# A decoder layer with routed experts: expert products scattered to token order by the tile and loaded plainly at the end, rows and sums in one buffer

## The chip, the cores and the metric

The kernel runs on one core of a Trainium2 chip. The metric is the time of one execution on the device in microseconds (us); the times shown are medians of several executions. A core has a matrix engine (TensorE, in profiles PE, with its weight loads listed apart as PEld), a vector engine (VectorE, DVE), a scalar engine (ScalarE, ACT), a general engine (GpSimd, POOL), and a queue engine (SyncE, SP) that issues transfers. Each engine takes its instructions in order; they wait for one another through semaphores. A transfer (DMA) issued by SP goes to one queue, one issued by POOL to others. An indirect transfer takes its row addresses from an index tile, one row for each of the 128 partitions.

## The reference

64 sequences of 128 tokens with 256 features go through one decoder layer, fp32 throughout: a state-space block, retention against a context, and a mixture of experts, each followed by a residual sum and a layer norm without gain. Cut to what matters:

```
x = _layernorm(x + attn(x))          # norm, W_in, conv, selective scan, W_out, + residual
x = _layernorm(x + xattn(x, ctx))    # q from x; k, v from ctx; scores * decay; no softmax
x = _layernorm(x + ffn(x))

def ffn(x):                          # shared expert + 2 of 8 routed experts per token
    shared = (silu(x @ sg.T) * (x @ su.T)) @ sd.T
    probs = sigmoid(x @ router_w.T + routing_bias)
    scores, indices = top_k(probs, 2)
    scores = scores / sum(scores, -1)
    w = zeros((t, 8)).at[arange(t)[:, None], indices].add(scores)
    g = silu(einsum('th,ehi->tei', x, gate_w)); u = einsum('th,ehi->tei', x, up_w)
    return shared + einsum('tei,eih,te->th', g * u, down_w, w)
```

## The kernel before

The rows of the decay table are equal in these inputs, so the function `_shared_decay` (L507) is used. The sequences are handled in 16 groups of 4 (512 tokens; a tile of a group is 128 partitions x 4 sequences x 256 features). The code is written as Python generators; `weave` (L1286) runs one as the main line and lets others step in between in proportion. The order so made is the order of each engine's queue.

**The loop** (L1319) has 17 ticks. Tick g runs the first half of group g (norm, input projection, convolution, scan), the second half of group g−1 (`after`: output projection, norm to x1, retention, norm to x2; then `route`), the shared expert of group g−2 (`early_shared`) unless the group is in `LATE` (groups 7 to 13), and expert tiles as far as their rows are known. `load_x` (L675) fetches x for the tick on POOL's queue with 2 buffers `xt`; the context tile `cT` is loaded in `after` (L857), also on POOL, and its buffer later holds the queries.

**Routing.** `route` picks two experts for each token, ranks the tokens of each expert, and scatters every x2 row to two rows of the DRAM array `xs`, which has one region for each expert: 8 indirect transfers a group (L1026), 128 in all. Positions are kept for the whole run in `index`, weights in `weight`. x2 of a late group, and x2 plus the shared expert's output of another, goes to the DRAM array `x2_rows`.

**Expert tiles.** `routed` runs 78 tiles: 57 of 256 rows, 21 of 128 rows. They become known in five batches (`BATCHES`, L41); `tile_list(k)` makes the list of batch k on the device: expert, first row, and whether new weights are needed. In the last batch each expert's last tile may be part empty, so the rows behind every expert's last are filled with zeros (L1098; the space behind the regions at the start, L621). For each tile `fetch` copies its entry (POOL, L1198), reads it into SP's registers, and loads the rows (L1201) and on a new expert 1.5 MB of weights (L1207). `hidden` transposes the rows, projects to gate and up, and multiplies; `down`, one tile later, projects down, copies the product out of PSUM (ACT, L1247) and stores it on SP to `ys` in tile order (L1248). 41 tiles run in the loop, 37 after it; with those `places` (L1156) steps along, which turns each scatter position in `index` into a row of `ys`.

**The last stage.** `all_shared` is the main line: for the 7 late groups it loads x2 back (`load_rows`, 4 buffers `x2_back`), transposes it and runs the shared expert. `all_sums` steps in between: for each group `combine` (L1264) gathers 8 times 128 rows of `ys` (POOL, L1270), each multiplied by its weight and added on DVE (L1274), then does the last layer norm into `o` and stores it. The 9 other groups come first in that list, the late ones follow as they are ready. `layernorm` (L626) takes statistics on DVE, one power on POOL (L636), one more on DVE, and applies the result on ACT a step later (L641).

PSUM has two pools: `gu` with 3 buffers for gate, up and the shared expert's output, `pm` with 5 for all else.

Of the kernel before, what the change touches and what calls it, by code (L numbers as in the profile page):

```python
# [42 lines left out]
NR = sum(n * r for _, _, n, r in BATCHES)  # L43
# [463 lines left out]
def _shared_decay(ctx, K):  # L507
# [84 lines left out]
    index = const.tile([P, NG * GB, 2], mybir.dt.int32, name="index")  # L592
    weight = const.tile([P, NG * GB, 2], F32, name="weight")

    x2_rows = dram.tile([NG, P, GB * D], F32, name="x2_rows", bufs=1)
    xs = dram.tile([NE * CAP + (NE - 1) * P, D], F32, name="xs", bufs=1)
    ys = dram.tile([NR, D], F32, name="ys", bufs=1)
# [13 lines left out]
    bounds = const.tile([P, NE, len(BATCHES)], F32, name="bounds")  # L611
    moves = const.tile([P, NE, len(BATCHES)], F32, name="moves")
    known = [0]
    weights = []
    for i in range(NW):
# [3 lines left out]
    zeros = const.tile([P, D], F32, name="zeros")  # L619
    nc.vector.memset(zeros, 0.0)  # L620
    nc.sync.dma_start(  # L621
        out=xs[NE * CAP :, :].rearrange("(i p) d -> p i d", p=P),
        in_=zeros.unsqueeze(1).to_broadcast([P, NE - 1, D]),
    )
# [50 lines left out]
    def load_x(g):  # L675
        xt = ring.tile([P, GB, D], F32, name="xt", bufs=2)
        nc.gpsimd.dma_start(out=xt, in_=x[g * GB : (g + 1) * GB].rearrange("b l d -> l b d"))
        return xt
# [173 lines left out]
    def after(g, st):  # L852
# [7 lines left out]
        x1 = one.tile([P, GB, D], F32, name="x1")  # L860
# [17 lines left out]
        def rotated(w, src, table, name, tag):  # L878

            ev = pm.tile([P, T], F32, name="pm")  # L880
            od = pm.tile([P, T], F32, name="pm")
            project(ev, w, 0, src)
            project(od, w, P, src)
            cos = rot_s[:, table, :].unsqueeze(1).to_broadcast([P, GB, L])
            sin = rot_s[:, table + 1, :].unsqueeze(1).to_broadcast([P, GB, L])
            r = one.tile([P, 2, T], F32, name=name, tag=tag)
            r0, r1 = seqs(r[:, 0, :]), seqs(r[:, 1, :])
            tmp = one.tile([P, GB, L], F32, name="tmp")
            nc.vector.tensor_tensor(r0, seqs(ev), cos, ALU.mult)
            nc.vector.tensor_tensor(tmp, seqs(od), sin, ALU.mult)  # L890
            nc.vector.tensor_tensor(r0, r0, tmp, ALU.subtract)
            nc.vector.tensor_tensor(r1, seqs(od), cos, ALU.mult)
            nc.vector.tensor_tensor(tmp, seqs(ev), sin, ALU.mult)
            nc.vector.tensor_tensor(r1, r1, tmp, ALU.add)
            return r
# [13 lines left out]
        qh = rotated(wq_s, x1T, 0, "qh", "cT")  # L909
# [9 lines left out]
        sc = one.tile([P, GB, L], F32, name="sc")  # L919
        nc.vector.tensor_tensor(sc, pss, dec.unsqueeze(1).to_broadcast([P, GB, L]), ALU.mult)  # L920
        yield
        x2 = ring.tile([P, GB, D], F32, name="x2", bufs=2)
# [10 lines left out]
        st["x2"] = x2  # L933

    writers = []

    def wrote(g, ins):

        tc.declare_no_dep(ins, group="scatters", reason="other rows")
        for k, (groups, *_) in enumerate(BATCHES):  # L940
            if groups <= g:
                tc.declare_no_dep(ins, group=f"fetches{k}", reason="other rows")
# [4 lines left out]
    def read(k, ins):  # L947

        tc.add_to_no_dep_group(f"fetches{k}", ins)
        for g in range(BATCHES[k][0], NG):  # L950
            tc.declare_no_dep(ins, group=f"scatters{g}", reason="other rows")
        for g, name in writers:
            if g < BATCHES[k][0]:
# [10 lines left out]
    def route(g, st):  # L964
# [46 lines left out]
        here = slice(g * GB, (g + 1) * GB)  # L1011
# [11 lines left out]
        nc.vector.tensor_copy(index[:, here, :], at)  # L1023
        for b in range(GB):
            for k in range(2):
                s = nc.gpsimd.indirect_dma_start(  # L1026
                    out=xs, in_=x2[:, b, :], in_offset=None,
                    out_offset=bass.IndirectOffsetOnAxis(ap=index[:, g * GB + b, k : k + 1], axis=0),
                )
                wrote(g, s.ins)  # L1030
        yield
# [6 lines left out]
        nc.vector.tensor_tensor(  # L1038
            weight[:, here, :], wk2, tot.unsqueeze(2).to_broadcast([P, GB, 2]), ALU.mult
        )  # L1040
        if g in LATE:
            nc.sync.dma_start(out=x2_rows[g], in_=x2.rearrange("p b d -> p (b d)"))
# [28 lines left out]
    def early_shared(g, st):  # L1071
        x2s = one.tile([P, GB, D], F32, name="x2s")
        yield from shared(st["x2"], st["x2T"], x2s)
        nc.sync.dma_start(out=x2_rows[g], in_=x2s.rearrange("p b d -> p (b d)"))

    def load_rows(g):
        t = late.tile([P, GB, D], F32, name="x2_back", bufs=4)
# [3 lines left out]
    def tile_list(k):  # L1081
# [5 lines left out]
        base = sum(m * r for _, _, m, r in BATCHES[:k])  # L1087
# [3 lines left out]
        if last:  # L1091

            behind = small.tile([P, NE], F32, name="behind", bufs=1)
            nc.vector.tensor_tensor(behind, pn, behind0, ALU.add)
            behind_i = small.tile([P, NE], mybir.dt.int32, name="behind_i", bufs=1)
            nc.vector.tensor_copy(behind_i, behind)
            for e in range(NE):
                s = nc.gpsimd.indirect_dma_start(  # L1098
                    out=xs, in_=zeros, in_offset=None,
                    out_offset=bass.IndirectOffsetOnAxis(ap=behind_i[:, e : e + 1], axis=0),  # L1100
                )
                wrote(groups - 1, s.ins)
# [18 lines left out]

        lo = bounds[:, :, k]
        nc.vector.tensor_tensor(lo, d, begin1, ALU.add)
        nc.vector.tensor_scalar(cum2[:, 0, :], cum0, float(size), float(base), ALU.mult, ALU.add)
        nc.vector.tensor_tensor(moves[:, :, k], cum2[:, 0, :], lo, ALU.subtract)
# [30 lines left out]
    def places():  # L1156

        n = NE * len(BATCHES)
        step = small.tile([P, n], F32, name="step", bufs=1)
        flat = moves.rearrange("p e k -> p (e k)")  # L1160
        nc.vector.tensor_copy(step[:, 0:1], flat[:, 0:1])
        nc.vector.tensor_tensor(step[:, 1:], flat[:, 1:], flat[:, 0 : n - 1], ALU.subtract)
        low = bounds.rearrange("p e k -> p (e k)")
        for g in range(NG):
            here = slice(g * GB, (g + 1) * GB)
            m = GB * 2
            was = small.tile([P, m], F32, name="was", bufs=1)
            nc.vector.tensor_copy(was, index[:, here, :].rearrange("p b k -> p (b k)"))
            over = small.tile([P, m, n], F32, name="over", bufs=1)
            nc.vector.tensor_tensor(  # L1170
                over, was.unsqueeze(2).to_broadcast([P, m, n]), low.unsqueeze(1).to_broadcast([P, m, n]), ALU.is_ge
            )
            nc.vector.tensor_tensor(over, over, step.unsqueeze(1).to_broadcast([P, m, n]), ALU.mult)
            by = small.tile([P, m], F32, name="by", bufs=1)
            nc.vector.tensor_reduce(by, over, AX.X, ALU.add)
            nc.vector.tensor_tensor(
                index[:, here, :].rearrange("p b k -> p (b k)"), was, by, ALU.add
            )
            yield

    def routed():
# [3 lines left out]
        def shape(i):  # L1185

            row = 0
            for k, (_, first, n, size) in enumerate(BATCHES):
                if i < first + n:
                    return k, size, row + (i - first) * size  # L1190
                row += n * size

        def fetch(i):

            k, size, _ = shape(i)
            t = tiles.tile([P, 2 * D + 4], F32, name="rows_in", bufs=3)
            entry = t[0:1, 2 * D : 2 * D + 3].bitcast(mybir.dt.int32)
            nc.gpsimd.tensor_copy(entry, what[:, i, :])  # L1198
            r = nc.sync.value_load(entry[:, 1:2], min_val=0, max_val=xs.shape[0] - size)
            t = t[:, 0 : size // P * D].rearrange("p (i d) -> p i d", d=D)  # L1200
# [12 lines left out]
        def hidden(i, t):  # L1213
            size = shape(i)[1]
# [8 lines left out]
            nc.scalar.copy(tT, ps)  # L1223
            yield
# [13 lines left out]
            return hid  # L1238

        def down(i, hid):  # L1240
            _, size, row = shape(i)
            wd = weights[i % NW][:, 2 * SZ :].rearrange("p (c h) -> p c h", c=CF)
            ps = pm.tile([P, size // P, D], F32, name="pm")
            for j in range(size // P):
                project_rows(ps[:, j, :], [h[:, j * P : (j + 1) * P] for h in hid], wd, slice(0, D))
            y = tiles.tile([P, size // P, D], F32, name="rows_out", bufs=2)
            nc.scalar.copy(y, ps)  # L1247
            nc.sync.dma_start(out=ys[row : row + size, :].rearrange("(j p) d -> p j d", p=P), in_=y)  # L1248

        ahead, waiting = [], None  # L1250
        for i in range(NT):
            if not ahead:
                ahead.append(fetch(i))
            hc = yield from hidden(i, ahead.pop(0))
            if waiting:
                down(*waiting)
            waiting = (i, hc)
# [6 lines left out]
    def combine(g, x2s):  # L1264

        for b in range(GB):
            s = g * GB + b
            for k in range(2):
                y = late.tile([P, D], F32, name="picked", bufs=12)
                nc.gpsimd.indirect_dma_start(  # L1270
                    out=y, out_offset=None, in_=ys,
                    in_offset=bass.IndirectOffsetOnAxis(ap=index[:, s, k : k + 1], axis=0),
                )
                nc.vector.scalar_tensor_tensor(  # L1274
                    x2s[:, b, :], y, weight[:, s, k : k + 1], x2s[:, b, :], ALU.mult, ALU.add
                )
            yield
        o = late.tile([P, GB, D], F32, name="o", bufs=2)
        yield from layernorm(o, x2s)
        nc.sync.dma_start(out=out[g * GB : (g + 1) * GB].rearrange("b l d -> l b d"), in_=o)  # L1280
# [67 lines left out]
    weave(rows, 6 * BATCHES[-2][2] + 4 * BATCHES[-1][2], (places(), NG, True))  # L1348
# [184 lines left out]
```

## Time and profile before

| what | value |
|---|---|
| median of 3 runs | 2128.95 us (2126.19 to 2129.11) |
| the profiled execution's own time | 2129.57 us |
| its span | 2127.9 us |
| PE busy | 1962.9 us (92%) |
| DVE, ACT, POOL busy | 1045.0, 744.4, 430.6 us |
| traffic | 244.85 MB, 115 GB/s in the mean |
| loop ends, about | 1530 us |
| tiles end, about | 1878.5 us |
| indirect transfers | 128 scatters of rows, 8 of zeros, 128 gathers |

The span is what the profile covers of the execution; the few tenths of a per cent around it are launch and end. In the page's second part each digit is the busy share of a fortieth of the span (53.2 us) in tenths. Groups name an instruction by line, engine and operation, output and inputs. The transfers that matter here, with KB each and the median time from issue to landing where it could be told:

```profile
xt<-in_x_dram POOLq DMA_DIRECT2D x16, 512.0 KB, 4.4
cT<-in_ctxT_dram POOLq DMA_DIRECT2D x16, 512.0 KB, 4.7
...
x_back<-x_rows SPq DMA_DIRECT2D x16, 512.0 KB
out_dram<-o SPq DMA_DIRECT2D x16, 512.0 KB
...
xs<-x,index POOLq DMA_INDIRECT x128, 2.5
picked<-ys,index POOLq DMA_INDIRECT x128, 2.8
```

POOL's longest waits, in total, times, and the longest one:

```profile
POOL rows_in L1198 <- PE pm L1221: 386.6, 44, 27.9
POOL cT L857 <- PE pm L914: 259.7, 9, 33.9
POOL cT L857 <- PE pm L1221: 193.8, 6, 32.3
...
POOL xt L677 <- DVE x L868: 72.1, 12, 19.9
```

### The profile page before, as it was taken

The page shows a single profiled execution, that of the slowest core. Times are in us where ns is not written, and L with a number is a line of the kernel's source. Part 1 is how long each engine was busy: PE and PEld are TensorE (multiplying, and loading weights), DVE is VectorE, ACT ScalarE, POOL GpSimd, SP SyncE. Part 2 cuts the span into 40 slices and gives each one's busy share as a digit, 9 for nine tenths or more (in the row PEclk, how much of TensorE's full clock was granted, in tenths as well). Part 3 has the DMA queues.
Part 4 walks back from the last instruction along what each step waited for, and adds up shares of the span by engine and source line. Part 5 has one row for each costly group of instructions (what it writes and reads, how often), then busy time and mean ns, then how long its engine had stood idle before and what let it go on. Part 6 is the DMA issues. An engine that isn't in the chain of part 4 may idle for free. (4 is left out here: it accounts for less than half of the span.)

```text
span 2127.9 us, 25170 instructions
## 1 busy us (share of the span) xinstructions
PE 1962.9 (92%) x8748; PEld 1420.9 (67%) x8748; DVE 1045.0 (49%) x2557; ACT 744.4 (35%) x1181; POOL 430.6 (20%) x504
## 2 busy tenths in 40 slices
PE   4799999999999999999999999999999998967767
PEld 1555666576766777776868676777878887844434
DVE  3666677565555655445555555454731111124453
ACT  2444344343342425353444435341211221212222
POOL 3031222121220202020211121110300000046671
PEclk9899999999999999999999999999999999999888
DMA  4111111331321334242524332233354567425441
GB/s 130 31 51 50 40 61 56 136 98 44 106 89 61 110 105 164 69 150 91 167 79 150 107 122 90 100 120 98 131 201 165 198 206 278 145 83 177 151 149 46
DMA packets 100888, 244.85 MB, mean 115 GB/s; under 512 B 23184, under 2 KB 68752, under 8 KB 91792
## 3 DMA queue, kind: packets, MB, share of 16 engines
q1 hardware_dynamic: 77968, 188.94, 26.6%
q0 software_dynamic: 17280, 51.40, 7.6%
q10 hardware_dynamic: 5504, 2.81, 0.5%
q8 instruction: 71, 1.16, 0.2%
q14 instruction: 65, 0.53, 0.1%
HBM read 202.48 MB, written 54.79 MB: 121 GB/s over the span
## 5 line engine op out<-in xcount | busy, mean ns | idle before, releaser
L664 PE MATMUL gu<-rows_T,routed_w 128*128 128x256 f32 (+1 forms) x2496 | 510.3, 356 | 9.1 <-ACT rows_T L1223 5.4
L664 PEld LDWEIGHTS gu<-rows_T,routed_w 128*128 128x128 f32 x2496 | 418.8, 192 | 77.4 <-issue 20.2
L1236 DVE TENSOR_TENSOR hid<-hid,gu 128x512 f32<-128x512 f32 x135 | 92.5, 685 | 358.6 <-PE gu L664 353.0
L664 PE MATMUL gu<-x2T,shared_w 128*128 128x512 f32 x512 | 239.4, 613 | 25.9 <-ACT x2T L652 16.2
L673 PE MATMUL pm<-routed_w,hid 128*128 128x256 f32 x1080 | 251.4, 381 | 11.6 <-DVE hid L1236 11.6
L664 PE MATMUL pm<-xnT,w_in_s 128*128 128x512 f32 x512 | 241.1, 597 | 0.7 <-ACT xnT L654 0.7
L673 PEld LDWEIGHTS pm<-routed_w,hid 128*128 128x128 f32 x1080 | 201.3, 190 | 46.0 <-DVE hid L1236 15.8
L664 PEld LDWEIGHTS gu<-x2T,shared_w 128*128 128x128 f32 x512 | 96.6, 195 | 142.6 <-issue 101.8
L702 DVE SCALAR_TENSOR_TENSOR xc<-pm,cw,xc 128x508 f32<-128x508 f32 (+2 forms) x192 | 140.3, 740 | 69.5 <-ACT xc L697 66.5
L1026 POOL DMA_INDIRECT xs<-x,index x128 | 137.4, 1073 | 170.6 <-DVE tot L1037 57.0
L1235 ACT ACTIVATE hid<-gu 128x512 f32<-128x512 f32 x135 | 80.4, 596 | 252.9 <-PE gu L664 252.7
L673 PE MATMUL gu<-shared_w,hc 128*128 128x256 f32 x512 | 128.3, 403 | 38.6 <-DVE hc L1058 38.6
L664 PEld LDWEIGHTS pm<-xnT,w_in_s 128*128 128x128 f32 x512 | 96.1, 192 | 84.1 <-issue 72.8
L1270 POOL DMA_INDIRECT picked<-ys,index x128 | 125.5, 981 | 104.7 <-DMA ys<-rows_out 31.0
L673 PEld LDWEIGHTS gu<-shared_w,hc 128*128 128x128 f32 x512 | 100.9, 202 | 64.7 <-DVE hc L1058 45.8
L1247 ACT COPY rows_out<-pm 128x512 f32<-128x512 f32 (+1 forms) x78 | 41.2, 528 | 265.7 <-PE pm L673 264.3
L1198 POOL COPY rows_in<-what 1x3 int32<-1x3 int32 x78 | 14.3, 188 | 502.1 <-PE pm L1221 386.6
L673 PE MATMUL pm<-w_out_s,sz 128*128 128x256 f32 x512 | 114.9, 380 | 0.4 <-DVE sz L848 0.3
L673 PEld LDWEIGHTS pm<-w_out_s,sz 128*128 128x128 f32 x512 | 96.5, 190 | 15.6 <-PE pm L841 1.3
L857 POOL DMA_DIRECT2D cT<-in_ctxT_dram x16 | 12.4, 776 | 453.5 <-PE pm L914 259.7
L636 POOL TENSOR_TENSOR rstd<-var,mhalf 128x4 f32<-128x4 f32 x64 | 65.9, 1030 | 166.2 <-DVE var L634 95.0
L697 ACT ACTIVATE xc<-pm,cb,cw 128x512 f32<-128x512 f32 x64 | 49.4, 773 | 112.5 <-PE pm L664 112.5
(225 smaller groups left out, 2629.9 us busy)
## 6 DMA issues: line engine op xcount, KB each, us to landing
routed_w<-in_ffn_dram SPq DMA_DIRECT2D x78, 1536.0 KB
rows_in<-xs SPq DMA_DIRECT2D x57, 256.0 KB
ys<-rows_out SPq DMA_DIRECT2D x57, 256.0 KB
xt<-in_x_dram POOLq DMA_DIRECT2D x16, 512.0 KB, 4.4
cT<-in_ctxT_dram POOLq DMA_DIRECT2D x16, 512.0 KB, 4.7
cq<-chunks SPq DMA_DIRECT2D x16, 512.0 KB
x_back<-x_rows SPq DMA_DIRECT2D x16, 512.0 KB
out_dram<-o SPq DMA_DIRECT2D x16, 512.0 KB
```

The costliest lines, as they stand in the source:

```text
L636: nc.gpsimd.tensor_tensor(rstd, var, mhalf, ALU.pow)
L664: nc.tensor.matmul(ps, lhsT=w[:, k, col : col + P], rhs=src[:, k, :], start=(k == 0), stop=(k == KD - 1),)
L673: nc.tensor.matmul(ps, lhsT=src[k], rhs=w[:, k, cols], start=(k == 0), stop=(k == chunks - 1))
L697: nc.scalar.activation(xcf[:, c, :], ps, AF.Identity, bias=cb[:, c : c + 1], scale=cw[:, c, TAPS - 1 : TAPS],)
L702: nc.vector.scalar_tensor_tensor(xc[:, c, :, s:], ps3[:, :, : L - s], cw[:, c, TAPS - 1 - s : TAPS - s], xc[:, c, :, s:], ALU.mult, ALU.add,)
L857: nc.gpsimd.dma_start(out=cT, in_=ctxT[:, g * T : (g + 1) * T].rearrange("(k p) t -> p k t", p=P))
L1026: s = nc.gpsimd.indirect_dma_start(out=xs, in_=x2[:, b, :], in_offset=None, out_offset=bass.IndirectOffsetOnAxis(ap=index[:, g * GB + b, k ...
L1198: nc.gpsimd.tensor_copy(entry, what[:, i, :])
L1235: nc.scalar.activation(hc, psg, AF.Silu)
L1236: nc.vector.tensor_tensor(hc, hc, psu, ALU.mult)
L1247: nc.scalar.copy(y, ps)
L1270: nc.gpsimd.indirect_dma_start(out=y, out_offset=None, in_=ys, in_offset=bass.IndirectOffsetOnAxis(ap=index[:, s, k : k + 1], axis=0),)
```

## The change

- **Rows carry their place.** A row of `xs` has 258 words: 256 features, the token's slot in `ys`, and its normalised weight. `route` holds two such row tiles, one for each expert choice: the tile that x1 and x2 are made in, and a copy `row1` (ACT). The scatters follow the weights, one step later than before. `index` lives for one group only; `weight` is gone.
- **Products go to token order.** `ys` has two rows for each token, in token order, and 15 x 128 rows of padding behind. Each tile copies slot and weight out of its rows (POOL, `to` and `wt`); `down` scales the product by the weight while it copies it (ACT, 128 rows at a time) and scatters it with one indirect transfer for each 128 rows (POOL), 135 in all, in place of the store on SP.
- **The last stage loads plainly.** `combine` loads 1 MB of `ys` for a group on SP (3 buffers), adds it in two DVE instructions, normalises in place and stores from there; `o` is gone. `x2_back` has 3 buffers.
- **Buffers.** x1, x2, the scattered row and the early groups' shared sum share one ring of 2 buffers (`x2`); `x2s` of the early groups is gone. The queries have a buffer of their own, `qh`; the masked scores share `tmp`. `xt` has 3 buffers.
- **Zero rows.** Empty rows need a slot of their own, in the padding, so that no two go to one place. `fill_behind` writes 15 blocks of zero rows after the loop, woven into the tiles; before each but the first, DVE adds 128 to the slots in the one tile `zeros`. The zero store at the start is gone. The last batch's fetches wait for these writes (`needs`).
- `places`, `bounds` and `moves` are gone.

The diff, cut to its core:

```diff
-    index = const.tile([P, NG * GB, 2], mybir.dt.int32, name="index")
-    weight = const.tile([P, NG * GB, 2], F32, name="weight")
+    slot = const.tile([P, NG * GB, 2], F32, name="slot")
+    nc.gpsimd.iota(slot, pattern=[[2 * L, NG * GB], [1, 2]], base=0, channel_multiplier=2,
...
-    xs = dram.tile([NE * CAP + (NE - 1) * P, D], F32, name="xs", bufs=1)
-    ys = dram.tile([NR, D], F32, name="ys", bufs=1)
+    xs = dram.tile([NE * CAP + (NE - 1) * P, DX], F32, name="xs", bufs=1)
+    ys = dram.tile([2 * 64 * L + (2 * NE - 1) * P, D], F32, name="ys", bufs=1)
...
-    nc.sync.dma_start(
-        out=xs[NE * CAP :, :].rearrange("(i p) d -> p i d", p=P),
-        in_=zeros.unsqueeze(1).to_broadcast([P, NE - 1, D]),
-    )
+    nc.gpsimd.iota(zeros[:, D : D + 1], pattern=[[0, 1]], base=2 * 64 * L, channel_multiplier=1,
...
-        xt = ring.tile([P, GB, D], F32, name="xt", bufs=2)
+        xt = ring.tile([P, GB, D], F32, name="xt", bufs=3)
...
-        x1 = one.tile([P, GB, D], F32, name="x1")
+        row = ring.tile([P, GB, DX], F32, name="x2", bufs=2)
+        x1 = row[:, :, 0:D]
...
-        qh = rotated(wq_s, x1T, 0, "qh", "cT")
+        qh = rotated(wq_s, x1T, 0, "qh", "qh")
...
-        x2 = ring.tile([P, GB, D], F32, name="x2", bufs=2)
+        x2 = x1
...
+    def needs(k):
+
+        return BATCHES[k][0] + (k == len(BATCHES) - 1)
...
+        rows = [st["row"], one.tile([P, GB, DX], F32, name="row1")]
+        nc.scalar.copy(rows[1][:, :, 0:D], x2)
...
+        for k in range(2):
+            nc.vector.tensor_copy(rows[k][:, :, D], slot[:, g * GB : (g + 1) * GB, k])
+            nc.vector.tensor_tensor(rows[k][:, :, D + 1], wk2[:, :, k], tot, ALU.mult)
+        yield
+        for k in range(2):
+            for b in range(GB):
+                s = nc.gpsimd.indirect_dma_start(
+                    out=xs, in_=rows[k][:, b, :], in_offset=None,
...
-        t = late.tile([P, GB, D], F32, name="x2_back", bufs=4)
+        t = late.tile([P, GB, D], F32, name="x2_back", bufs=3)
...
+    def fill_behind():
+        for j in range(2 * NE - 1):
+            if j:
+                nc.vector.tensor_scalar(
+                    zeros[:, D : D + 1], zeros[:, D : D + 1], float(P), None, ALU.add
+                )
+            if j < NE:
+                s = nc.gpsimd.indirect_dma_start(
+                    out=xs, in_=zeros, in_offset=None,
+                    out_offset=bass.IndirectOffsetOnAxis(ap=behind_i[:, j : j + 1], axis=0),
+                )
+            else:
+                row = NE * CAP + (j - NE) * P
+                s = nc.sync.dma_start(out=xs[row : row + P, :], in_=zeros)
+            wrote(NG, s.ins)
             yield
...
+            to = tiles.tile([P, size // P], mybir.dt.int32, name="to", bufs=3)
+            nc.gpsimd.tensor_copy(to, t[:, :, D])
+            wt = tiles.tile([P, size // P], F32, name="wt", bufs=3)
+            nc.gpsimd.tensor_copy(wt, t[:, :, D + 1])
...
-            nc.scalar.copy(y, ps)
-            nc.sync.dma_start(out=ys[row : row + size, :].rearrange("(j p) d -> p j d", p=P), in_=y)
+            for j in range(size // P):
+                nc.scalar.activation(y[:, j, :], ps[:, j, :], AF.Copy, scale=wt[:, j : j + 1])
+                s = nc.gpsimd.indirect_dma_start(
+                    out=ys, in_=y[:, j, :], in_offset=None,
+                    out_offset=bass.IndirectOffsetOnAxis(ap=to[:, j : j + 1], axis=0),
+                )
...
     def combine(g, x2s):
-        for b in range(GB):
-            s = g * GB + b
-            for k in range(2):
-                y = late.tile([P, D], F32, name="picked", bufs=12)
-                nc.gpsimd.indirect_dma_start(
-                    out=y, out_offset=None, in_=ys,
...
+        y = late.tile([P, GB, 2, D], F32, name="picked", bufs=3)
+        nc.sync.dma_start(
+            out=y, in_=ys[g * GB * 2 * L : (g + 1) * GB * 2 * L, :].rearrange(
+                "(b p k) d -> p b k d", p=P, k=2)
+        )
+        yield
+        for k in range(2):
+            nc.vector.tensor_tensor(x2s, x2s, y[:, :, k, :], ALU.add)
+        yield
+        yield from layernorm(x2s, x2s)
+        nc.sync.dma_start(out=out[g * GB : (g + 1) * GB].rearrange("b l d -> l b d"), in_=x2s)
+        yield
```

## The prediction

> **What bounds the kernel now.** I read the page's busy rows first, then windows by stage, then the waits and the timeline of TensorE (PE) in the stage where it stops being busy.
>
> ```profile
> PE   4799999999999999999999999999999998967767
> POOL 3031222121220202020211121110300000046671
> PEclk9899999999999999999999999999999999999888
> ```
>
> PE is at 9 in nearly every slice of the loop and below it in the first slices and the last six, where POOL rises to 7. Windows put microseconds on the stages (columns: length, busy time of PE, its weight loads, DVE, ACT, POOL, granted clock, DMA share, GB/s):
>
> ```profile
> 0.00:95.00 95.00, 53.10 (x183) 30.70 (x184) 41.16 (x103) 32.24 (x48) 21.87 (x43) 0.91 0.30 90
> 95.00:1530.00 1435.00, 1403.44 (x6220) 1003.60 (x6219) 832.27 (x2008) 586.33 (x891) 257.12 (x277) 0.99 0.30 97
> ...
> 1560.00:1878.50 318.50, 303.96 (x1740) 268.54 (x1739) 37.12 (x54) 64.38 (x127) 5.97 (x34) 0.99 0.55 189
> 1878.50:2128.00 249.50, 172.44 (x504) 98.16 (x502) 110.32 (x330) 56.25 (x107) 142.19 (x144) 0.87 0.41 128
> ```
>
> The loop leaves PE idle 31.6 us of 1435 and the tile stage 14.5 of 318.5; both are bound by PE. The last stage (249.4 us to the span's end at 2127.9) leaves it idle 77. What PE waits for there (total, times, longest):
>
> ```profile
> PE gu L673 <- DVE hc L1058: 37.7, 9, 11.8
> PE gu L664 <- ACT x2T L652: 16.2, 4, 9.2
> PE gu L664 <- DVE hc L1058: 5.3, 4, 2.9
> PE gu L664 <- ACT hc L1057: 4.3, 2, 3.1
> ```
>
> Sum 63.5. The product hc on DVE is late because DVE is in order and stands behind the multiply-adds of L1274, which wait for gathers that POOL issues singly:
>
> ```profile
> L1270 POOL DMA_INDIRECT picked<-ys,index x128: 942/953/1340, 1881.5 to 2094.7; - x128
> ```
>
> Issuing spans 213 of the stage's 249 us. The timeline shows a late group after a wait and the last, undisturbed one (start, length, what is waited for in brackets):
>
> ```profile
> 2033.81 10.51 PE L664 MATMUL gu<-x2T,shared_w 128*128 128x512 f32 x20 [9.17 <-ACT x2T L652]
> ...
> 2092.61 0.82 PE L650 MATMUL pm<-ident,x_back 128*128 128x128 f32 x6
> 2093.67 14.00 PE L664 MATMUL gu<-x2T,shared_w 128*128 128x512 f32 x32 [0.24 <-ACT x2T L652]
> 2107.50 7.07 PE L673 MATMUL gu<-shared_w,hc 128*128 128x256 f32 x32
> ```
>
> An undisturbed group takes 2092.61 to 2114.57, 21.96 us, so seven need 153.7. After PE's end 13.3 us remain (2114.6 to 2127.9: add, statistics, power on POOL, ACT, store). The rest, 249.4 − 153.7 − 63.5 − 13.3 = 18.9 us, is the clock: the same 20 matmuls that take 8.75 undisturbed take 10.51 after the 9.17 wait. Six waits exceed 4 us (11.79, 9.17, 7.12, 6.72, 5.27, 4.82), so each costs 3.15 us more than itself. [...]
>
> **The change, part by part.** (1) The last stage. 128 gathers and 128 multiply-adds (0.48 us, 61 us of DVE) go. Each of 16 groups instead gets one plain 1 MB load on SP and two DVE adds of 128x1024, 1.23 us each by this row:
>
> ```profile
> L811 DVE TENSOR_TENSOR eq<-eq,cq x16: 1211/1226/1226, 65.1 to 1420.8; 128x1024 f32<-128x1024 f32 x16
> ```
>
> That is 39 us of DVE; POOL keeps 16 powers. The trace has no 1 MB load; a 512 KB one lands in 4.4 to 4.7 us (x and context loads), a 1.5 MB one moved at 300 to 400 GB/s, so I take 6, bounds 4.7 and 9.4. The end after PE: the adds (2.45) were spread over the gathers and now precede the statistics, 13.3 becomes 15.5.
>
> What is left of waits I worked from the order of the built program on each queue. The sum now lies in its load buffer until its output store has landed, and there are three such buffers, not four, shared with the late groups' reloads. So a late group's reload stands in SP's queue behind a store that waits for: load of products, two adds, statistics, power, four ACT passes (2.3 us), which ACT takes behind the hc activations. Store 4.5 and reload 4.7 make a turn of 9.2; part of it lies beside the 22 us of the previous group. By group: the first waits 1.3 (hc behind adds whose load is new), the second 6, the third 6.8, the fourth 1, the fifth 7 (two waits), the others none: 22.1. Three of these exceed 4 us: 3 × 3.15 = 9.5. Stage: 153.7 + 15.5 + 22.1 + 9.5 = 200.8, against 249.4: −48.6.
>
> (2) Products scattered. The tile's row copy (L1247, 0.585 us of ACT) becomes two passes of half size, about equal; 78 SP stores become 135 indirect writes on POOL, plus 156 small copies of address and weight. The nearest row:
>
> ```profile
> L1026 POOL DMA_INDIRECT xs<-x,index x128: 956/969/2122, 138.2 to 1523.7; - x128
> ```
>
> 0.96 with 0.30 between issues is 1.26; 135 are 170 us of POOL: 82 (103 us) in the loop, where POOL is busy 257 of 1435, 53 (67 us) in the tile stage, where it is busy 6. PE sets the pace of both, and it hides them. Without that cover: each scatter waits on POOL for ACT's scaled copy of the previous tile, and behind it wait the power of the layer norms (then ACT, then PE) and the entry copies (then SP's fetch, a tile or more ahead). I take +3, bounds 0 and +15 (46 us of idle PE grown by a third). [...]
>
> (3) Route: one ACT copy of 128x1024 (1.06) per group, three more small DVE operations, scatters one step later. About 1.7 us × 16 of ACT and DVE, off PE's path, since rows are read a batch later: 0, and inside (2)'s bounds otherwise.
>
> (4) The fill behind the last rows: 15 writes in one chain, each with a DVE add that waits for the previous write to land (2.4 by the zero write's row, and the add): 14 × 2.8 = 39 us. DVE is in order, so a tile's hid product can wait 2.5 us behind such an add; PE has three gate/up buffers in hand and an up projection of ~4 us ahead, which hide most. I take +2, bounds 0 and +12.
>
> (5) Start: 896 KB of zeros leave the queue ahead of the first x load, which is issued at 18.3 and lands at 26.1 while DMA moves 290 to 415 GB/s: 2.6 us less at 350, the new iota and constants about 0.4, and PE waits on that load. I take −1.5, bounds −2.5 and +0.5.
>
> (6) At nothing: 16 steps of DVE that turn scatter positions into product positions go, in a stage where DVE is 12% busy under PE. The queries' own buffer and the third x buffer release the context and x loads earlier; the waits they end are POOL's (454 us on cT, 72 on xt), and neither load is in PE's list. Bounds −3 (a tenth of the loop's 31.6 us of idle PE) and 0. Shared buffers for x1, x2 and the row: two in the ring, as x2 had; bounds 0 and +6, if the x1 of a tick waits for the scatters two groups back.
>
> Sum: −48.6 + 3 + 2 − 1.5 = −45.1, so the span goes from 2127.9 to 2082.8. The median shown, 2128.95, is 1.05 above that span (the profiled execution's own time, 2129.57, is 1.67 above): **2084**.
>
> **Rivals.** *A clean last stage.* Reloads run far enough ahead and nothing waits: 153.7 + 15.5 = 169.2, the span 2127.9 − 249.4 + 169.2 + 3.5 = 2051.2, time 2052. For it: DMA share is only 0.41 there. Against it: three buffers and stores ahead of loads in one queue. *The loads' wait takes the gathers' place.* Six late groups each wait a full turn of 9.2, with or without 3.15 of clock: 55 to 74 on top of 169.2, time 2108 to 2126, middle 2117. For it: a PE wait on x2T of 9.17 exists already, with four buffers. Against: early groups are few per late group (nine to seven). *Slower.* POOL is in order, and the 82 scatters in the loop hold back the powers that feed ACT and PE. The gain of 48 is gone when this idles PE more than 45 of their 103 us, 0.55 us a scatter; at 0.9 each, 74 us, the time is 2084 − 3 + 74 = 2155. For it: POOL's power already stands in the loop with a scatter ahead of it; against: POOL waits there for hundreds of us, so it has slack. *The change does not do what it says:* the order of the built program has no gather left, so I give this nothing.
>
> **How the numbers follow.** Forecast 0.62, clean stage 0.13, loads' wait 0.16, slower 0.09. The predicted time is 2084. Its own unknowns (4.7 to 9.4 for a load is ±5 over the waits, the bounds of (2), (4), (6)) give 2070 to 2108 for it alone. The range takes most of the clean stage and most of the loads' wait: 2053 to 2118. A difference under 0.2% (4 us) can't be told from none. Slower than that: 0.08 of the slower rival; within: 0.03, from the top of the loads' wait and the edge of the slower rival; faster: 0.89.
>
> **What would show it.** Right: POOL without a gather after the tiles, a last stage near 200 us with PE's waits near 22, the largest on x2T behind a reload; windows of the loop and tile stage within 5 us of before; POOL some 170 us busier by its scatters. Wrong: a loop longer by tens of us with PE waiting on ACT passes of the norms (slower rival), hid products late behind the fill's adds, or nine or more waits on x2T in the last stage.

## The result, and the profile after

The changed kernel takes 2132.46 us (median of 9 runs, 2129.24 to 2134.73) beside 2126.19 for the kernel before, measured with it (9 runs): a ratio of 1.0024, 95% interval 1.0013 to 1.0034. It is slower by a quarter of a per cent, where 2084 was forecast and 2118 was the range's upper end.

The last stage did what was forecast; the loop and the stretch right behind it gave all of it back. First the busy rows of the page of the changed kernel:

```profile
PE   4789899999898999999999999999989999888987
...
DVE  3665665765555565545555654554431111113563
...
POOL 3021221211202131313131222213131222221010
```

POOL's peak at the end is gone and PE's dip there is shallower. In exchange slices 3, 5, 11 and 13, in the loop's first part, and slice 30, at its end, fall from 9 to 8. Windows of the changed kernel (columns as in the prediction: length, busy PE, weight loads, DVE, ACT, POOL, clock, DMA share, GB/s), cut at the same places of the program as those below of the kernel before:

```profile
97.50:843.00 745.50, 702.59 (x2923) 469.71 (x2922) 440.10 (x1055) 293.08 (x453) 150.72 (x175) 0.98 0.23 73
843.00:1440.00 597.00, 579.66 (x2678) 435.89 (x2678) 316.68 (x767) 269.39 (x414) 152.63 (x208) 0.99 0.35 115
...
1578.00:1641.00 63.00, 51.38 (x193) 35.78 (x192) 9.81 (x24) 9.43 (x18) 11.94 (x19) 0.92 0.47 154
1641.00:1938.50 297.50, 284.26 (x1664) 252.58 (x1662) 35.08 (x51) 67.32 (x139) 67.36 (x154) 1.00 0.55 190
1938.50:2130.80 192.30, 158.74 (x496) 92.11 (x496) 96.55 (x234) 56.16 (x106) 19.64 (x17) 0.93 0.50 168
```

```profile
95.00:798.00 703.00, 688.02 (x2922) 460.96 (x2921) 439.82 (x1039) 282.94 (x435) 132.47 (x133) 1.00 0.24 76
798.00:1393.00 595.00, 581.19 (x2677) 438.23 (x2676) 320.11 (x752) 257.58 (x384) 96.70 (x113) 0.99 0.36 116
...
1530.00:1578.00 48.00, 48.00 (x195) 35.35 (x194) 26.57 (x68) 8.66 (x15) 3.78 (x8) 1.00 0.56 201
```

The same 2922 matmuls that took 703 us take 745.5, with PE idle 43 us in place of 15. The other 14.6 us are the matmuls themselves, 702.6 us in place of 688.0, at a granted clock of 0.98 in place of 1.00: a third of the loss is clock. In the changed kernel's window it is 0.50 in six stretches (158.5 to 165.4, 240.5 to 247.3, 329.2 to 332.6, 404.3 to 407.7, 578.4 to 581.8 and 677.4 to 684.2), in the window before in none; each begins in a wait of PE of 5.4 to 6.1 us, or within 0.2 us after waits of 3.1 to 3.7 us in sum. PE is busy 24.4 us in them, so by an estimate from these figures they make about 12 of the 14.6. The second half of the loop costs 2 us more; the 48 us from the 41st tile on, with the last group's shared expert in them, become 63. A ledger from landmarks in the two traces (first statistics of each tick, first transposes of each tile, last down projection) accounts for the spans, 2127.9 and 2130.8. The third column is the variant without the two losses that the experiments find, from a batch of runs in which the kernel before takes 2127 us:

| stretch | before | changed | both edits (`e3_again`) |
|---|---|---|---|
| start to the first statistics | 26.3 | 24.3 | 25.8 |
| ticks 0 to 7 | 673.8 | 719.5 | 675.6 |
| rest of the loop, to its last tile (the 41st) | 829.6 | 834.1 | 833.0 |
| that tile to the 42nd | 31.8 | 47.4 | 31.5 |
| the other tiles | 317.0 | 312.2 | 311.9 |
| last stage | 249.4 | 193.3 | 195.5 |

What DVE waits for in the changed kernel has a line that the kernel before has not (total, times, longest):

```profile
DVE hid L1222 <- PE gu L663: 323.5, 88, 7.2
DVE row L1037 <- DMA xs<-row,index: 137.9, 15, 14.0
DVE shift L637 <- POOL rstd L635: 74.5, 63, 3.6
...
DVE zeros L1153 <- DMA xs<-zeros,behind_i: 31.5, 8, 7.2
...
DVE zeros L1153 <- DMA xs<-zeros: 12.6, 6, 3.4
```

L1037 is the copy of the slots into the row buffer, 0.17 us each. It reads a constant and writes `row1`, which has one buffer, so it depends on nothing but that the previous group's rows have left that buffer. The weaving fixes the order of most instructions, as the section on the kernel tells, but not of one like this: in the built program it stands far ahead of its own group's routing (that it is put where its buffer may come free is an inference from the times that follow). The first two such copies start at 16.9 and 17.0 us, before any group has been computed, and each later one of `row1` runs 12 to 17 us after the weights of the previous group's rows are written on DVE (L1038). The buffer is not free when DVE comes to it. The copy for the other choice, whose tile has two buffers, waits 2.2 us in all. The timeline of DVE, PE and POOL of the changed kernel at one such place (start, length, wait in brackets):

```profile
233.85 0.74 DVE L844 SCALAR_TENSOR_TENSOR xc<-xc,dsk,pm 128x512 f32<-128x512 f32 x1
234.48 0.97 POOL L1042 DMA_INDIRECT xs<-row,index  x1 [0.31 <-issue]
...
238.30 0.97 POOL L1042 DMA_INDIRECT xs<-row,index  x1 [0.30 <-issue]
240.92 0.17 DVE L1037 COPY row<-slot 128x4 f32<-128x4 f32 x1 [6.33 <-DMA xs<-row,index]
241.00 0.68 DVE L847 TENSOR_TENSOR sz<-sz,xc 128x512 f32<-128x512 f32 x1
...
241.74 1.65 PE L672 MATMUL pm<-w_out_s,sz 128*128 128x256 f32 x3 [6.14 <-DVE sz L847]
```

The four scatters of `row1` are issued one behind the other on POOL, the last at 238.30; it lands at 240.80; DVE, idle 6.33 us, does 0.17 us of copying for a group whose own `row1` is scattered 74 us later, then the product sz of this group, for which PE has waited 6.14 us. The wait for one instruction is a wait of the whole queue behind it. Over the whole run PE's waits on sz and mt, the two products that stand there in five of ticks 0 to 7, are these, in the changed kernel and then in the kernel before:

```profile
PE pm L672 <- DVE sz L847: 13.1, 5, 6.1
...
PE pm L840 <- DVE mt L826: 12.4, 4, 5.7
```

```profile
PE pm L841 <- DVE mt L827: 1.1, 2, 0.6
...
PE pm L673 <- DVE sz L848: 0.3, 1, 0.3
```

The waits of PE in the changed kernel's last stage:

```profile
PE pm L649 <- DMA x_back<-x_rows: 7.0, 2, 4.7
PE gu L663 <- ACT x2T L651: 6.3, 5, 4.2
PE gu L672 <- DVE hc L1065: 3.2, 3, 1.9
PE gu L663 <- DVE hc L1065: 2.3, 1, 2.3
```

18.8 us, where the kernel before had 63.5.

### The profile page after: what moved, and what is told of

It reads as the page before. It is cut to its first block, busy times and chain, and to the rows that moved or that the text cites. A ratio compares the mean times of both kernels' runs of the same rounds, so it can differ in the third digit from the quotient of the medians.

```text
span 2130.8 us, 25083 instructions
## 1 busy us (share of the span) xinstructions
PE 1963.9 (92%) x8748; PEld 1419.6 (67%) x8748; DVE 1001.5 (47%) x2426; ACT 775.9 (36%) x1254; POOL 462.9 (22%) x669
## 4 chain that ended last, share of the span: by engine, by line
PE 70%; DVE 9%; DMA 7%; ACT 5%; POOL 4%; issue 4%; SPq 0%; DVEq 0%; POOLq 0%; ACTq 0%
PE gu L663 24%; PE pm L672 17%; PE pm L663 15%; PE pm L717 2%; POOL xs L1042 2%; PE gu L672 2%; PE pm L649 2%; PE pm L840 2%; DMA xs<-row,index 1%; PE pm L914 1%; PE pm L927 1%; PE pm L1203 1%; DMA x_back<-x_rows 1%; POOL rstd L635 1%; DMA routed_w<-in_ffn_dram 1%
## 5 line engine op out<-in xcount | busy, mean ns | idle before, releaser
L1235 POOL DMA_INDIRECT ys<-rows_out,to x135 | 133.7, 991 | 346.8 <-ACT rows_out L1234 310.3
L1234 ACT ACTIVATE rows_out<-pm,wt 128x256 f32<-128x256 f32 x135 | 57.8, 471 | 266.3 <-PE pm L672 245.6
L672 PE MATMUL pm<-w_out_s,sz 128*128 128x256 f32 x512 | 121.7, 394 | 13.2 <-DVE sz L847 13.1
L672 PE MATMUL gu<-shared_w,hc 128*128 128x256 f32 x512 | 118.9, 382 | 5.5 <-DVE hc L1065 5.5
L672 PEld LDWEIGHTS gu<-shared_w,hc 128*128 128x128 f32 x512 | 95.1, 190 | 27.4 <-DVE hc L1065 8.7
L1042 POOL DMA_INDIRECT xs<-x,index x64 | 66.2, 1034 | 126.3 <-DVE row L1038 49.5
L640 ACT ACTIVATE x<-x,shift,rstd 128x256 f32<-128x256 f32 x128 | 67.9, 590 | 57.3 <-DVE shift L637 57.3
L1205 ACT COPY rows_T<-pm 128x512 f32<-128x512 f32 (+1 forms) x78 | 41.2, 528 | 130.3 <-PE pm L1203 130.3
```

The lines of the kernel that those rows point to most:

```text
L640: nc.scalar.activation(dst[:, b, :], src[:, b, :], AF.Identity, bias=shift[:, b : b + 1], scale=rstd[:, b : b + 1])
L672: nc.tensor.matmul(ps, lhsT=src[k], rhs=w[:, k, cols], start=(k == 0), stop=(k == chunks - 1))
L1042: s = nc.gpsimd.indirect_dma_start(out=xs, in_=rows[k][:, b, :], in_offset=None, out_offset=bass.IndirectOffsetOnAxis(ap=index[:, b, k : k ...
L1234: nc.scalar.activation(y[:, j, :], ps[:, j, :], AF.Copy, scale=wt[:, j : j + 1])
L1235: s = nc.gpsimd.indirect_dma_start(out=ys, in_=y[:, j, :], in_offset=None, out_offset=bass.IndirectOffsetOnAxis(ap=to[:, j : j + 1], axis=0),)
```

## The experiments

They ran in three batches, in which the kernel before takes 2173, 2127 and 2162 us; each result therefore stands as a ratio to the kernel before in its own batch. The expectations of the first batch are in microseconds and were made for a kernel before of 2126; they are read as ratios to it, too (2080 to 2095 is 0.978 to 0.985). The expectations speak of different chips, but the first two batches carry the same chip number, so it is not shown that the chip makes the difference; that its transfers are slower, as one of them has it, was the author's assumption, and no run shows it.

**The slot column written late (`e1_slot_late`, `e1_again`).**

```diff
-            nc.vector.tensor_copy(rows[k][:, :, D], slot[:, g * GB : (g + 1) * GB, k])
+            nc.vector.scalar_tensor_tensor(
+                rows[k][:, :, D], tot, 0.0, slot[:, g * GB : (g + 1) * GB, k], ALU.mult, ALU.add
+            )
```

> The slot column is written by an instruction that also reads the reciprocal sum (times 0), so it can't stand in DVE's queue ahead of the group's own routing. Theory (in the changed kernel DVE stands at the slot copy of the next group until the previous group's second row buffer has been scattered: 15 waits, 137.9 us, of which the first eight ticks let 45 us through to PE): these waits go and the first eight ticks return to within 1 us of their lengths before the change; 2132.5 - 45 = 2087, 2080 to 2095. Rival one (the ring of two buffers shared by x1, x2, row and sum, or the longer route with its ACT copy, makes the ticks long): the waits go but the ticks stay long, 2122 or more. Rival two (the products' scatters on POOL): only the ticks without tiles (the first four, 25 us) recover, about 2107.

2125.61 us beside 2173.16, ratio 0.9774 (0.9748 to 0.9801), as much as expected or slightly more.

> The slot column behind the routing, alone, a second time: the first was on the chip whose kernel before took 2173 us. Theory: against the changed kernel, whose ratio to the kernel before is 1.0024 to 1.0034, 45 us of the first eight ticks go and the fill's 16 stay: 0.980 to 0.984 of the kernel before. Rival (most of the 57 us that both edits saved is the fill's): 0.99 or more.

2118.74 beside 2161.94, ratio 0.9801 (0.9778 to 0.9824). The same number of instructions of the same 0.17 us, and the kernel is about 2% faster than the kernel before. The profile of the second run has these instructions, and no idle time before them:

```profile
L1037 DVE SCALAR_TENSOR_TENSOR x<-tot,slot x16: 146/166/168, 142.8 to 1542.6; 128x4 f32<-128x4 f32 x16
L1037 DVE SCALAR_TENSOR_TENSOR row<-tot,slot x16: 147/166/168, 143.5 to 1542.7; 128x4 f32<-128x4 f32 x16
```

The first now starts at 142.8. Ticks 0 to 7 of the second run take 92, 73, 72, 72, 84, 93, 94 and 98 us, where the changed kernel has 95, 81, 82, 76, 84, 95, 102 and 105 and the kernel before 91, 73, 73, 72, 81, 93, 95 and 97: 42 of the 45.7 us are back, the idle time and the clock behind it: PE is idle 33.4 us in these ticks (61.5 in the changed kernel, 30.7 before), and its 2653 matmuls take 643.7 us (658.0, and 643.1 before). The 3 us of tick 4 are not back, and were not followed up. The rivals fall: ticks with and without tiles recover, and the shared buffers, the longer route and the fill's chain are still there.

**Filler rows without a chain (`e2_fill`, `e2_again`).** All 15 slot columns lie side by side in one tile, and each write takes its own window of it.

```diff
-    zeros = const.tile([P, DX], F32, name="zeros")
+    zeros = const.tile([P, D + 2 * NE], F32, name="zeros")
...
-            if j:
-                nc.vector.tensor_scalar(
-                    zeros[:, D : D + 1], zeros[:, D : D + 1], float(P), None, ALU.add
-                )
+            block = zeros[:, j : j + DX]
```

> The 15 blocks of filler rows are cut from one tile that holds all 15 slot columns, so no DVE addition waits for the previous block to land; the rows' other words are any finite numbers, since their products go to padding. Theory (the chain of 14 landings at the end of the loop lengthens the stretch between the last two tiles of the loop and the first behind it from 31 to 47 us): 16 less, 2116, 2112 to 2121; DVE's 44 us of waits there go. Rival (the stretch is long because the first products behind the loop wait on POOL, or for other reasons of the loop's end): 2128 or more.

2152.77 beside 2173.16, ratio 0.9907 (0.9875 to 0.9939), more than expected.

> The filler blocks without a chain, alone, a second time. Theory: 16 of the 57 to 62 us, 0.993 to 0.997 of the kernel before. Rival: 0.985 or less.

2151.99 beside 2161.94, ratio 0.9948 (0.9933 to 0.9963), as expected. In both profiles the stretch from the 41st tile to the 42nd is 31.5 and 31.4 us, as before the change, and DVE's waits there are gone, while with the slot edit alone, where the chain stays, the stretch is 42.4 and 45.8; that part is settled. The two intervals overlap only at 0.994, so the size of the gain as a ratio is less sure than its place. The changed kernel's timeline shows how the chain stood in the way:

```profile
1588.67 0.96 POOL L1157 DMA_INDIRECT xs<-zeros,behind_i  x1 [2.36 <-DVE zeros L1153]
...
1595.61 0.15 DVE L1153 TENSOR_SCALAR zeros<-zeros 128x1 f32<-128x1 f32 x1 [7.21 <-DMA xs<-zeros,behind_i]
1596.04 0.98 POOL L1157 DMA_INDIRECT xs<-zeros,behind_i  x1 [3.57 <-DVE zeros L1153]
...
1598.81 0.15 DVE L1153 TENSOR_SCALAR zeros<-zeros 128x1 f32<-128x1 f32 x1 [3.05 <-DMA xs<-zeros,behind_i]
1598.91 0.69 DVE L1222 TENSOR_TENSOR hid<-hid,gu 128x512 f32<-128x512 f32 x1
...
1599.65 1.22 PE L663 MATMUL gu<-x2T,shared_w 128*128 128x512 f32 x1 [7.72 <-DVE hid L1222]
```

Two additions stand in a row ahead of one product; DVE waits 7.21 and 3.05 us, PE 7.72. This PE wait alone is half of the 16 us; the rest is smaller waits (4.6 us) and the clock, 0.92 in the window from 1578 to 1641, where PE's busy time is 3.4 us longer than in the same stretch before.

**Both edits (`e3_both`, `e3_again`), and the changed kernel beside them (`e0_after`).**

> Both edits. If the two losses are independent: 2132.5 - 45 - 16 = 2071, 2064 to 2079. What would then be left against the kernel before is the last stage (57 us shorter as profiled) and 1 to 4 us of the loop for the scatters. If they share a cause, or the time is taken by something behind them, the sum is smaller: 2080 or more.

2124.39 beside 2173.16, ratio 0.9763 (0.9736 to 0.9789): only 1.2 us under the slot column alone in the same batch.

> The changed kernel itself, so that it stands beside its variants and the kernel before on one chip: the four runs before this one were on a chip whose kernel before took 2173 us. Theory: 1.002 of the kernel before, as measured first, whatever the chip; if the chip's slower transfers weigh on the kernel before more than on the changed one, below 0.995.

2133.42 beside 2127.20, ratio 1.0034 (1.0023 to 1.0045). In the other two batches the changed kernel was not run.

> Slot column behind the routing and filler blocks without a chain, as in the run with both edits. Theory (45 us in the first eight ticks, 16 at the loop's end): 57 to 65 us less than the changed kernel on the same chip, 0.971 to 0.976 of the kernel before. Rival (part of the gain was this other chip's): under 45 us.

2076.24 beside the same 2127.20, ratio 0.9765 (0.9742 to 0.9788): 57 us under the changed kernel. The ledger's third column is this run: against the changed kernel the ticks give 43.9 us back and the stretch behind the 41st tile 15.9, so here the two losses nearly add up. The first batch doesn't confirm it. There the second edit shortens the stretch as well, from 42.4 to 31.4 us, but the rest of the loop grows from 872.1 to 882.4 us. In that batch it takes 870 to 882 us in every profile, against 833 to 839 in the batch at 2127, by waits of another kind (last section). Each loss and its place is shown; that the two savings add is shown in one batch only.

**Every product scatter twice (`e5_double`).**

```diff
+                s = nc.gpsimd.indirect_dma_start(
+                    out=ys2, in_=y[:, j, :], in_offset=None,
+                    out_offset=bass.IndirectOffsetOnAxis(ap=to[:, j : j + 1], axis=0),
+                )
```

> Both edits, and every scatter of products issued twice on POOL, the second time to a DRAM array that nothing reads: 135 more indirect transfers, 170 us of POOL at 0.96 + 0.30. Theory (PE's pace covers them): at most 6 us more than with both edits, all of it in the loop. Rival (in-order POOL hands their time on, as the prediction's slower case had it, 0.5 us a scatter or more): 65 us more or above, with PE waiting behind the layer norms' powers.

2093.09, ratio 0.9845 (0.9829 to 0.9861): 17 us more than with both edits, between the two expectations. That is 0.125 us a scatter. So the second set of scatters is covered for nine tenths of its 1.26 us each of POOL. The profiled run, the fastest of the four and 12 us longer in its span than that of both edits, has 7 of them between the first and the 41st tile and 5 in the other tiles, where the expectation put all in the loop. Through which wait they come is not settled: no line of PE's waits grew by more than 4 us.

**Two x buffers, queries in the context's buffer (`e6_xq`).**

```diff
-        xt = ring.tile([P, GB, D], F32, name="xt", bufs=3)
+        xt = ring.tile([P, GB, D], F32, name="xt", bufs=2)
...
-        qh = rotated(wq_s, x1T, 0, "qh", "qh")
+        qh = rotated(wq_s, x1T, 0, "qh", "cT")
```

> Both edits, with two x buffers again and the queries in the context's buffer again. Theory (neither ends a wait that PE sees): within 4 us of the run with both edits, POOL's waits on cT and xt back in the hundreds of us. Rival (the earlier x and context loads help the first ticks): 8 us slower or more, in the first ticks.

2076.84, ratio 0.9771 (0.9755 to 0.9787), the same as with both edits: these two buffers bring nothing measurable. The expectation's other half fails: POOL's wait for cT didn't come back, since it had never gone (216 us in 8 waits here, 242 in 15 with a buffer of its own), and its waits for xt are 33 us in both.

**The last stage's buffers (`e4_back5`, `e4_again`), and its stores on ACT (`e8_actstore`).**

```diff
-        t = late.tile([P, GB, D], F32, name="x2_back", bufs=3)
+        t = late.tile([P, GB, D], F32, name="x2_back", bufs=5)
...
-        y = late.tile([P, GB, 2, D], F32, name="picked", bufs=3)
+        y = late.tile([P, GB, 2, D], F32, name="picked", bufs=2)
```

> As with both edits, and the last stage's buffers divided anew in the same space: 5 for the rows loaded back, 2 for the products (3 and 3 in the changed kernel). Theory (late groups' reloads wait for an early group's output store to free a buffer; PE waits 13.3 us on the reload and its transposed copy, and clock behind it): 10 to 16 us less than with both edits, 2055 to 2061. Rival (products' loads become late with two buffers, and the wait moves to hc): within 4 us of the run with both edits, or slower.

2110.04 beside 2173.16, ratio 0.9712 (0.9669 to 0.9755): 14.4 us under both edits in the same batch, as expected.

> Both edits, 5 buffers for the rows loaded back and 2 for the products, a second time. Theory (PE's waits on reloads, 6.4 in the last stage of the run with both edits, the products waiting behind, and their clock): 8 to 14 us under both edits, 0.970 to 0.973 of the kernel before. Rival: 0.976, as with both edits.

2097.79 beside 2161.94, ratio 0.9712 (0.9690 to 0.9734), half a per cent under the ratio of both edits, in the range expected. The last stage is 178.0 us in the second run's profile. PE's waits from the last tiles on:

```profile
PE gu L663 <- ACT x2T L651: 5.2, 4, 2.9
PE gu L672 <- DVE hc L1067: 3.3, 3, 1.9
PE pm L672 <- DVE hid L1221: 1.5, 2, 0.8
PE gu L663 <- DVE hc L1067: 0.6, 1, 0.6
```

The wait for the reload itself is gone, so it was the buffers.

```diff
-        nc.sync.dma_start(out=out[g * GB : (g + 1) * GB].rearrange("b l d -> l b d"), in_=x2s)
+        nc.scalar.dma_start(out=out[g * GB : (g + 1) * GB].rearrange("b l d -> l b d"), in_=x2s)
```

> As the run before it, with the outputs' stores issued by ACT, behind the passes that make them, so that no load of SP's queue stands behind a store that waits. Theory (what is left of the waits in the last stage, 9 us and their clock, comes from the buffers and from order on DVE, not from SP's queue): within 3 us of the run before it. Rival (SP's queue order keeps reloads back): 5 to 9 us less.

2100.88, ratio 0.9724 (0.9703 to 0.9744), not to be told from the run before it: with five buffers SP's queue order costs nothing. `e4_again` is the fastest version found, 2.9% under the kernel before.

## Why the prediction was wrong

**Bounds now: right.** The last stage was the only one not bound by PE, and the gathers were its cause: PE's waits there fell from 63.5 to 18.8 us when they went.

**Step (1), the last stage: right, a little low.** Forecast 200.8 (−48.6), measured 193.3 (−56.1). PE's waits were 18.8 against 22.1, two of them above 4 us against three. The clock cost 5.0 (PE busy 158.74 against 7 x 21.96) where 9.5 was put: 2.5 for each long wait, where 3.15 was taken. Up to PE's end in this stage of the changed kernel the granted clock is 0.50 from 1964.2 to 1971.0, from 2001.8 to 2005.2 and from 2046.2 to 2053.0, two stretches of 6.8 us and one of 3.4; the short one stands behind a wait of only 2.3 us, so counting the waits above 4 us, as the forecast did, doesn't give these stretches. The end after PE was 192.3 − 158.7 − 18.8 = 14.8 against 15.5.

**Step (2), the scatters: the size right, as far as it can be told.** +3 was taken, bounds 0 and +15. With both edits the first eight ticks are 1.8 us longer than before the change, the rest of the loop 3.4 longer and the tile stage 5.1 shorter. The doubling gives 17 for a second set of 135, 2 above the upper bound; whether the first set costs less, or is paid for by what was gained in the tile stage, was not separated. The products' scatters took about as long as the rows' did before: the changed kernel's 135 took 0.954 to 1.317 us, median 0.976, the loop's included, where the 128 before took 0.956 to 2.122, median 0.969. The longest scatter of rows in the changed kernel took 1.98 us, and no run tells why.

**Step (3), route: this is the step that failed.** The prediction put the three more small DVE operations "off PE's path, since rows are read a batch later: 0". It priced their length and asked who reads their result. It did not ask what they wait for, what stands behind them on DVE, nor where in the queue they stand. Ticks 0 to 7 grew by 45.7 us, and 42 of them go when the copies can no longer run ahead, as the first experiment shows. Seven of the 15 waits lie in these ticks, 49 us together. The other eight are longer, 89 us together, and cost little (4.5 us over the whole rest of the loop, all causes together). So the average, 9.2 us a wait, says little. That PE's other work covers the later waits is argued, not shown: ticks 9 to 16 have four expert tiles each. Some tiles are not enough, for ticks 6 and 7 have two each and grew by 7 and 8 us, nearly as much as ticks 1 and 2, which have none.

**Step (4), the fill: mechanism right, size wrong.** Forecast +2, upper bound +12, measured 15.6. The waits' sum was nearly right (44 us against 39). The cover was not: all 14 additions stand between 1567 and 1621, in places two in a row ahead of a product, and single landings took up to 6.8 us against the 2.4 that was used, the median of a row whose own longest was 6.3.

**Steps (5) and (6): right.** The first statistics start 2.0 us earlier (−1.5 forecast); the buffers of the queries and of x are worth nothing (`e6_xq`).

The forecast was −45.1. Replacing the two wrong terms (+45.7 in place of 0, +15.6 in place of +2) gives +14; the last stage's 7.5 below forecast and 4.8 from the tile stage bring it to +2, against 2.9 measured. The slower rival had the place right, POOL's in-order scatters in the loop, and the mechanism wrong: it named the products' scatters and the layer norms' powers. It was the scatters of the rows, which are as many as before the change, and a DVE copy that waits for their landing. Its point of decision, 45 us more of idle PE in the loop, was not reached: PE's idle time there grew by 34 us (65.5 in place of 31.6), and by 12 right behind it; the rest of the loss is clock.

## What to carry to other kernels

An instruction that depends only on a constant and a free buffer can be placed far ahead of its work; in the order of its engine's queue it then holds up what stands behind it until the buffer's last reader has finished, here an indirect transfer (at 240.92 DVE idle 6.33 us, and PE 6.14 for the product behind it; 15 such waits of DVE, 137.9 us). Price an added instruction by what it waits for and what is queued behind it, not by its duration, and read the built order of its engine for instructions that start long before their results are needed (16.9 us here, for a group whose rows are scattered from 146.8 on). Making the instruction read a value that is computed late cost nothing here (0.17 us each, as before) and fixed its place.

## What the runs showed of the hardware that was not expected

The landing of the products' scatters took 2.4 to 8.0 us, median 6.0, where the rows' and gathers' medians were 2.5 and 2.8 before. And batches of runs differ: the kernel before took 2126 to 2173 us, while the ratios of one kernel in two batches had overlapping intervals (0.9763 and 0.9765, 0.9712 twice, 0.9774 and 0.9801, 0.9907 and 0.9948). The profiles of both edits show where: in the batch at 2173 the rest of the loop takes 882 us, in that at 2127 833, and in these stretches PE's waits put to the expert tiles' transposed rows (rows_T) are 26.1 us in place of 5.5. Whether the chip or the time of the run makes the difference is open.
